# Regrouping the eight PSUM banks of the second half of an attention and mixture-of-experts kernel

## The chip, the cores and the metric

The kernel runs on one core of a Trainium2 chip. The metric is the device time of the program in microseconds, the median of several executions.

## The reference

The input is `x` of shape (2, 1024, 512) in float32: two sequences of 1024 tokens, 2048 tokens in all, each with 512 features. A vector per sequence, `c`, is multiplied with a matrix to give six modulation rows (shift, scale and gate for each of two halves).

The first half is a linear-attention layer: layer norm with modulation, a projection to queries, keys and values, a rotation of keys and values, a sum over all tokens of the products of normalized keys and values, and an output projection, added back through a gate.

The second half is a mixture of experts. With `h` the normalized and modulated tokens:

```
scores = softmax(h @ gate_w)                  # 8 experts, the best 2 of each token are used
g      = silu(h @ w_gate[e]) * (h @ w_up[e])  # hidden size 352, for each chosen expert e
routed = sum over the 2 experts of weight * (g @ w_down[e])
shared = (silu(h @ sw_gate) * (h @ sw_up)) @ sw_down      # hidden size 704, all tokens
out    = x + gate * (routed + shared)
```

## The kernel before, in words

Tokens are handled in 16 tiles of 128 (numbered `t`), and in four groups of four tiles (numbered `g`, 0 to 3). The first half of the program makes attention for all tokens, and, woven into it, the shared expert's hidden layer of group 0. What the change touches comes after that, in this order on TensorE:

1. **The rest of the shared expert for groups 0 and 1.** `shared_down(0, ...)` multiplies group 0's hidden layer with `sw_down`. Then `half_up(1, ...)` makes the last half chunk of group 1's hidden layer (tile `ph`, L1345), five calls of `seven(n, 1, ...)` make its five whole chunks, and `shared_down(1, ...)` makes its output (tiles `sd`, L928). `keep_shared` (L1044 on VectorE, L1045 on GpSimd) takes each output tile out of PSUM.
2. **The routed blocks.** Tokens sorted by expert are handled in blocks of 128 rows. Block `i` loads its rows (`hb`, L1417) and its expert's three weight matrices (`wg_r`, `wu_r`, `wd_r`), transposes the rows (`tr_b`, L337), makes two products (`bg` and `bu`, L1458), the gate on ScalarE and VectorE (L1336 to L1338), turns the result (`gtr`, L1470) and makes the output (`by`, L1486), which ScalarE copies out (L1490). How many blocks there are depends on the data: at least `NB0` = 32 and at most 39. The first 32 are plain code. Each later one stands in `tc.If(blocks > i)`, and the last block's output in `tc.If(blocks == i)` (L1578 and L1580), then `tc.If(blocks >= NB1)` (L1583) and one large conditional for the rest (L1586). In the profiled run 35 blocks are made, so blocks 32, 33 and 34 are in conditional code that runs, and the conditionals of L1583 and L1586 are passed by.
3. **The shared expert for groups 2 and 3.** Five pairs of `seven(n, 2, ...)` and `seven(n, 3, ...)`, two `half_up`, two `shared_down`. Between them VectorE adds the routed rows to the tokens (`next_sum`, L1377 to L1385).

`seven` makes a pair of 128x512 products with seven multiplications of 128x256 instead of eight (L1016). Each multiplication has two matmul instructions (one for each half of the inner dimension). They lie in four PSUM banks: `m1, m2` share one, `m6, m7` one, `m5, m3` one, and `m4` has one for itself. ScalarE copies `m1` (L1024), VectorE adds the others up (L1026 to L1034), ScalarE makes the sigmoid (L1036), VectorE multiplies (L1037, L1038).

From the second group of the shared expert on, the eight PSUM banks are two pools. A tile takes the next buffer of its pool in turn, and its first matmul waits until the earlier tile in that buffer has been read:

```python
    ps_mm = ctx.enter_context(tc.tile_pool(name="ps_mm2", bufs=5, space=PSUM))
    ps_tr = ctx.enter_context(tc.tile_pool(name="ps_tr2", bufs=3, space=PSUM))
```

`mm_ps` (five banks) holds `ph`, the three paired products of `seven`, and `bg`, `bu` and `by` of a block. `tr_ps` (three banks) holds `m4`, the outputs `sd` of `shared_down`, and the transposes `tr_b` and `gtr`.

The order of the instructions on each engine is not the order of the source. A scheduler lays them out when the program is built, by its own estimates of when operands and buffers are free. It can put an instruction ahead of others of its engine, also out of a later stage; it doesn't move one that touches a buffer which a conditional writes past that conditional. On the chip each engine then takes its instructions in the fixed order.

The weights of groups 2 and 3's shared expert are loaded a second time. Their first four chunks go into `s_again` (L1311), two transfers of 1 MB each, which SyncE issues among the first blocks' weights.

Of the kernel before, what the change touches and what calls it, by code (L numbers as in the profile page):

```python
# [8 lines left out]
FP = mybir.dt.float32  # L9
# [5 lines left out]
PSUM = bass.MemoryType.PSUM  # L15
# [3 lines left out]
P = 128  # L19
# [5 lines left out]
def kernel(  # L25
# [22 lines left out]
    E, _, H = w_gate.shape  # L48
# [4 lines left out]
    NS = NT // 4  # L53
# [32 lines left out]
    ps_mm = psums.enter_context(tc.tile_pool(name="ps_mm", bufs=3, space=PSUM))  # L86
    ps_tr = psums.enter_context(tc.tile_pool(name="ps_tr", bufs=2, space=PSUM))
# [9 lines left out]
    def mm_ps(name):  # L97
        return ps_mm.tile([P, 512], FP, tag="mm", name=name)

    def tr_ps(name):  # L100
        return ps_tr.tile([P, 512], FP, tag="tr", name=name)
# [5 lines left out]
    def act_tile(home, name):  # L107
# [11 lines left out]
        out=before_t,  # L119
# [687 lines left out]
    gTs = {}  # L807
# [92 lines left out]
    def shared_weights():  # L900

        tiles = [weight_tiles(f"s{i}a") for i in range(2)]
        wgu = []
        for i, (wg, wu, wd) in enumerate(tiles):
            views = []
            for w, src in ((wg, sw_gate), (wu, sw_up)):
                v = w.rearrange("p k h -> p (k h)").rearrange("p (k h) -> p k h", k=KH)
                nc.sync.dma_start(
                    v, src.rearrange("(k p) h -> p k h", p=P)[:, i * KH : (i + 1) * KH, :]
                )  # L910
                views.append(v)
            wgu.append(views)
        wds = load_down([wd for _, _, wd in tiles])

        def up_part(which, i, h0, m):
            return wgu[i][which][:, :, h0 : h0 + m]

        return up_part, wds

    def shared_down(g, gT, wds, use, ps_of, apart=False):  # L920


        for j0 in range(0, 4, 2):
            pss = [ps_of(f"sd_{g}_{j0 + i}") for i in range(2)]

            def chunk(i, c):
                rows = slice(i * HP, (i + 1) * HP) if c == NF else slice(0, P)
                nc.tensor.matmul(  # L928
                    pss[i],
                    gT[rows, c, (j0 + i) * P : (j0 + i + 1) * P],  # L930
                    wds[c][rows, :],
                    start=(c == 0),
                    stop=(c == NF),
                )

            if apart and j0 == 2:
                for i in range(2):
                    for c in range(NF + 1):
                        chunk(i, c)
            else:  # L940
                for i in range(2):
                    for c in range(NF):
                        chunk(i, c)
                    if i == 0:
                        yield
                for i in range(2):
                    chunk(i, NF)
            for i in range(2):
                use(g * 4 + j0 + i, pss[i])
            yield  # L950
# [37 lines left out]
    def mix_weights(n, up_part, store):  # L988

        a11, a12, a21, a22 = (  # L990
            up_part(w, i, n * P, P) for w in range(2) for i in range(2)
        )
        store = [v.rearrange("p (k h) -> p k h", k=KH) for v in store]
        s1, s2, s4 = store[0:3]
        s3 = store[3] if len(store) > 3 else a21
        nc.vector.tensor_add(s1, a21, a22)
        nc.vector.tensor_sub(s2, s1, a11)
        nc.vector.tensor_sub(s3, a11, a21)
        nc.vector.tensor_sub(s4, a12, s2)
        return a11, a12, a22, s1, s2, s3, s4  # L1000

    def seven(n, g, weights, b):

        a11, a12, a22, s1, s2, s3, s4 = weights
        c1, c2 = (
            gpool.tile([P, 2 * TH], FP, tag="sg", bufs=8, name=f"c{i}_{n}_{g}")
            for i in range(2)
        )
        (c11, c12), (c21, c22) = ((c[:, 0:TH], c[:, TH:]) for c in (c1, c2))

        def products(ps, *pairs):
            halves = []
            for i, (w, h) in enumerate(pairs):
                half = ps[:, i * TH : (i + 1) * TH]
                for k in range(KH):
                    nc.tensor.matmul(  # L1016
                        half, w[:, k, :], h[:, k, :], start=(k == 0), stop=(k == KH - 1)
                    )
                halves.append(half)
            return halves  # L1020

        add = nc.vector.tensor_add
        m1, m2 = products(mm_ps(f"m12_{n}_{g}"), (a11, b.b11), (a12, b.b21))
        nc.scalar.copy(c11, m1)  # L1024
        m6, m7 = products(mm_ps(f"m67_{n}_{g}"), (s2, b.t2), (s3, b.t3))
        add(c12, c11, m6)  # L1026
        add(c11, c11, m2)
        add(c22, c12, m7)
        m5, m3 = products(mm_ps(f"m53_{n}_{g}"), (s1, b.t1), (s4, b.b22))
        (m4,) = products(tr_ps(f"m4_{n}_{g}"), (a22, b.t4))  # L1030
        add(c12, c12, m5)
        add(c12, c12, m3)
        add(c21, c22, m4)
        add(c22, c22, m5)  # L1034
        dst = gTs[g][:, n, :]
        on_act = nc.scalar.activation(dst, c1, AF.Sigmoid)  # L1036
        nc.vector.tensor_mul(dst, dst, c1)  # L1037
        return on_act, nc.vector.tensor_mul(dst, dst, c2)  # L1038
# [227 lines left out]
    up_part, wds = shared_weights()  # L1266
# [26 lines left out]
    hroom.close()  # L1293
    attn.close()
    psums.close()
    ps_mm = ctx.enter_context(tc.tile_pool(name="ps_mm2", bufs=5, space=PSUM))
    ps_tr = ctx.enter_context(tc.tile_pool(name="ps_tr2", bufs=3, space=PSUM))


    gpool = ctx.enter_context(tc.tile_pool(name="gpool", bufs=1, side="right", reuse_waits="tile"))  # L1300
# [13 lines left out]
    def shared_again(firsts):  # L1314
        tiles = [weight_tiles(f"s{i}b") for i in range(2)]
        rests = []
        for w, src in zip(tiles[0], (sw_gate, sw_up)):
            v = w.rearrange("p k h -> p (k h)")[:, 0 : KC * (HS - HB)].rearrange(
                "p (k h) -> p k h", k=KC
            )  # L1320
            nc.sync.dma_start(v, src.rearrange("(k p) h -> p k h", p=P)[:, :, HB:HS])
            rests.append(v)
        wds = load_down([wd for _, _, wd in tiles])

        def up_part(which, i, h0, m):
            if h0 < HB:
                w = firsts[which]
            else:
                w, h0 = rests[which], h0 - HB
            return w[:, i * KH : (i + 1) * KH, h0 : h0 + m]  # L1330

        return up_part, wds
# [67 lines left out]
    for n in range(NF):  # L1400
        seven(n, 1, ready.pop(n), toks[1])
        if n + 2 < NF:
            ready[n + 2] = mix_weights(n + 2, up_part, s_stores[n % 2])
    for _ in shared_down(1, gTs[1], wds, keep_shared, tr_ps):
        pass


# [73 lines left out]
        return gtT  # L1481

    def block_out(i, gtT, w):
        ps = mm_ps(f"by_{i}")
        for c, (_, m) in enumerate(HCH):
            nc.tensor.matmul(  # L1486
                ps, gtT[:m, c, :], w[2][:m, c, :], start=(c == 0), stop=(c == NH - 1)
            )
        y = rpool.tile([P, D], FP, tag="y", name=f"y_{i}")
        nc.scalar.copy(y, ps)  # L1490

        queue = nc.sync if i + 1 < NB0 else nc.scalar
        queue.dma_start(ybuf[i * P : (i + 1) * P, :], y)
# [21 lines left out]
    def finish_block(i):  # L1515
        block_out(i, turned[i], weights[i])
# [83 lines left out]
    up_part, wds = shared_again(firsts)  # L1600
# [22 lines left out]
    for n in range(NF):  # L1623
        for g in last:
            after = seven(n, g, ready[n], toks[g])

            if n:
                next_sum(after)
        if n == 1:
            with tc.issue_after(after[1].ins):  # L1630
                ready[NF - 1] = mix_weights(NF - 1, up_part, quarters(s_last))
# [2 lines left out]
        next_sum()  # L1634
    spare = act_tile(4, "spare_again")
    for g in last:
        for _ in shared_down(g, gTs[g], wds, finish, tr_ps, apart=(g == NS - 1)):
            pass


# [67 lines left out]
```

## Time and profile before

| what | value |
|---|---|
| median of 3 runs | 771.56 us (768.81 to 772.03) |
| the profiled execution's own time | 772.12 us |
| its span, first to last instruction | 770.3 us |
| mean granted TensorE clock | 0.994 |
| TensorE busy | 751.9 us, 98% of the span |
| VectorE busy | 428.7 us, 56% |
| ScalarE busy | 232.5 us, 30% |
| GpSimd busy | 214.9 us, 28% |
| HBM traffic | 128.15 MB read, 30.16 MB written |

A timeline row gives the start, the length, the engine (PE is TensorE's matmul, PEld its weight load, DVE VectorE, ACT ScalarE, SPq the queue of SyncE), the source line, the operation, the tiles out and in, and how many executions the row merges. In brackets stands the idle time of the engine before it and what ended it. A float32 matmul instruction shows as two executions. Rows of matmuls overlap, since their ends are modelled: the distance between starts is the better measure. In a table of stretches each engine's busy time is followed by the number of instructions, then come the granted clock (PEclk; 1.00 is full), the share in which the DMA engines were busy, and GB/s.

### The profile page before, as it was taken

The page shows a single profiled execution, that of the slowest core. Times are in us where ns is not written, and L with a number is a line of the kernel's source. Part 1 is how long each engine was busy: PE and PEld are TensorE (multiplying, and loading weights), DVE is VectorE, ACT ScalarE, POOL GpSimd, SP SyncE. Part 2 cuts the span into 40 slices and gives each one's busy share as a digit, 9 for nine tenths or more (in the row PEclk, how much of TensorE's full clock was granted, in tenths as well). Part 3 has the DMA queues.
Part 4 walks back from the last instruction along what each step waited for, and adds up shares of the span by engine and source line. Part 5 has one row for each costly group of instructions (what it writes and reads, how often), then busy time and mean ns, then how long its engine had stood idle before and what let it go on. Part 6 is the DMA issues. An engine that isn't in the chain of part 4 may idle for free. (4 is left out here: it accounts for less than half of the span.)

```text
span 770.3 us, 8477 instructions
## 1 busy us (share of the span) xinstructions
PE 751.9 (98%) x2527; PEld 415.8 (54%) x2527; DVE 428.7 (56%) x979; ACT 232.5 (30%) x495; POOL 214.9 (28%) x241
## 2 busy tenths in 40 slices
PE   7999999999999999999999999999999998999997
PEld 2444444444444444684565656656566554888542
DVE  3888956898736888982222123222221121499964
ACT  4664523557643153110122122221221212122310
POOL 1234524863632687562100000000000000234530
PEclk9999999999999999999999999999999999999999
DMA  8950001212335711367999999999999884624551
GB/s 322 383 170 16 14 0 69 109 57 67 137 96 195 269 68 42 123 260 252 337 352 347 348 344 334 343 339 325 330 338 331 292 287 161 193 83 136 166 163 55
DMA packets 96369, 158.91 MB, mean 206 GB/s; under 512 B 8089, under 2 KB 51097, under 8 KB 96321
## 3 DMA queue, kind: packets, MB, share of 16 engines
q1 hardware_dynamic: 89984, 138.41, 53.6%
q0 software_dynamic: 5760, 18.88, 7.4%
q10 hardware_dynamic: 576, 1.05, 0.4%
q8 instruction: 22, 0.36, 0.2%
q14 instruction: 27, 0.21, 0.1%
HBM read 128.15 MB, written 30.16 MB: 206 GB/s over the span
## 5 line engine op out<-in xcount | busy, mean ns | idle before, releaser
L1360 POOL DMA_INDIRECT y<-ybuf,yrows x32 | 37.0, 1156 | 336.0 <-SPq L1586 288.4
L410 PE MATMUL kv<-w_kv,xnT 128*128 128x512 f32 x256 | 115.2, 596 | 0.5 <-ACT xnT L393 0.5
L1486 PE MATMUL by<-wd_r,gtT 128*128 128x512 f32 (+1 forms) x210 | 96.1, 593 | 0.8 <-DVEq L1578 0.8
L1458 PE MATMUL bg<-wg_r,hbT 128*128 128x352 f32 x280 | 88.9, 460 | 0.9 <-ACT y L1490 0.9
L1458 PE MATMUL bu<-wu_r,hbT 128*128 128x352 f32 x280 | 88.5, 459 | 0.0
L410 PEld LDWEIGHTS kv<-w_kv,xnT 128*128 128x128 f32 x256 | 46.9, 190 | 57.2 <-issue 48.1
L1458 PEld LDWEIGHTS bu<-wu_r,hbT 128*128 128x128 f32 x280 | 53.2, 190 | 29.6
L1473 DVE COPY gtT<-gtr 128x256 f32<-128x256 f32 x35 | 14.9, 425 | 97.0 <-PE gtr L1470 97.0
L1458 PEld LDWEIGHTS bg<-wg_r,hbT 128*128 128x128 f32 x280 | 50.4, 190 | 23.5 <-ACT y L1490 1.3
L571 PE MATMUL o<-wp,xnT 128*128 128x512 f32 x128 | 57.3, 593 | 0.0
L1337 DVE TENSOR_TENSOR sg_b<-sg_b,bg 128x352 f32<-128x352 f32 x35 | 18.3, 521 | 68.8 <-ACT sg_b L1336 68.8
L1486 PEld LDWEIGHTS by<-wd_r,gtT 128*128 128x128 f32 (+1 forms) x210 | 37.2, 191 | 34.5 <-issue 33.5
L1450 ACT COPY hbT<-tr_b 128x512 f32<-128x512 f32 x36 | 21.1, 586 | 101.1 <-PE tr_b L337 101.1
L1338 DVE TENSOR_TENSOR gt<-sg_b,bu 128x352 f32<-128x352 f32 x35 | 18.3, 521 | 47.2 <-PE bu L1458 47.2
L1490 ACT COPY y<-by 128x512 f32<-128x512 f32 x35 | 20.5, 586 | 70.7 <-PE by L1486 48.9
L571 PEld LDWEIGHTS o<-wp,xnT 128*128 128x128 f32 x128 | 23.8, 190 | 28.6 <-issue 27.0
L1336 ACT ACTIVATE sg_b<-bg 128x352 f32<-128x352 f32 x35 | 16.2, 464 | 76.1 <-PE bg L1458 76.1
L440 POOL TENSOR_TENSOR cross<-kv 128x128 f32<-128x128 f32 x16 | 12.6, 790 | 75.4 <-DVE kv L417 45.2
L530 PE MATMUL wp<-aw,wqT 128*128 128x512 f32 x64 | 30.0, 625 | 0.7 <-DVE aw L511 0.7
L433 ACT ACTIVATE sq<-kv 128x512 f32<-128x512 f32 x32 | 20.2, 630 | 27.2 <-DVE kv L417 25.6
L610 POOL TENSOR_TENSOR hr<-hr,cb 128x512 f32<-128x512 f32 x16 | 22.3, 1393 | 21.3 <-issue 7.2
L393 ACT ACTIVATE xnT<-tr_a,colsb 128x128 f32<-128x128 f32 x64 | 24.4, 455 | 11.0 <-PE tr_a L337 10.9
(319 smaller groups left out, 1264.7 us busy)
## 6 DMA issues: line engine op xcount, KB each, us to landing
wg_r<-in_w_gate_dram SPq DMA_DIRECT2D x35, 704.0 KB
wu_r<-in_w_up_dram SPq DMA_DIRECT2D x35, 704.0 KB
wd_r<-in_w_down_dram SPq DMA_DIRECT2D x35, 512.0 KB
hb<-hbuf SPq DMA_DIRECT2D x36, 256.0 KB
ybuf<-y SPq DMA_DIRECT2D x31, 256.0 KB
wd_r<-in_w_down_dram SPq DMA_DIRECT2D x35, 192.0 KB
wmod<-in_wmod_dram SPq DMA_DIRECT2D x6, 1024.0 KB
x<-in_x_dram SPq DMA_DIRECT2D x3, 1024.0 KB
```

Source lines behind the costliest of these rows:

```text
L393: turned1[t] = nc.scalar.activation(xnT[g][:, f, j * P : (j + 1) * P], ps[:, f * P : (f + 1) * P], AF.Identity, bias=colsb[:, 1, f : f + 1 ...
L410: nc.tensor.matmul(ps, xnT[g][:, k, j * P : (j + 1) * P], w_kv[:, i, k, :], start=(k == 0), stop=(k == KC - 1),)
L433: nc.scalar.activation(sq, kv[:, i, :], AF.Square, accum_out=ss[:, i : i + 1])
L530: nc.tensor.matmul(ps, wqT[:, k, f * P : (f + 1) * P], aw[:, k, :], start=(k == 0), stop=(k == KC - 1),)
L571: nc.tensor.matmul(ps, xnT[g][:, k, j * P : (j + 1) * P], wp[:, k, :], start=(k == 0), stop=(k == KC - 1),)
L610: nc.gpsimd.tensor_mul(h, h, cb1[b])
L1337: nc.vector.tensor_mul(sg[:m, :n], sg[:m, :n], pg[:m, :n])
L1360: nc.gpsimd.indirect_dma_start(out=y, out_offset=None, in_=ybuf, in_offset=bass.IndirectOffsetOnAxis(ap=yrows[:, t, s : s + 1], axis=0), b ...
L1450: nc.scalar.copy(hbT.rearrange("p k q -> p (k q)"), ps)
L1458: nc.tensor.matmul(ps[:, :H], hbT[:, k, :], wt[:, k, :], start=(k == 0), stop=(k == KC - 1))
L1486: nc.tensor.matmul(ps, gtT[:m, c, :], w[2][:m, c, :], start=(c == 0), stop=(c == NH - 1))
L1490: nc.scalar.copy(y, ps)
```

## The change

The eight banks become four pools of two: `mm_ps` keeps `ph`, `m5`/`m3`, `bg` and `bu`; `tr_ps` keeps `m4`, `tr_b` and `gtr`; `out_ps` takes `m6`/`m7` and the block outputs `by`; `start_ps` takes `m1`/`m2`. The output tiles `sd` of `shared_down` take two from `start_ps` and two from `tr_ps` in turn. No tile that is made inside a conditional comes from `start_ps`.

```diff
-        m1, m2 = products(mm_ps(f"m12_{n}_{g}"), (a11, b.b11), (a12, b.b21))
+        m1, m2 = products(start_ps(f"m12_{n}_{g}"), (a11, b.b11), (a12, b.b21))
         nc.scalar.copy(c11, m1)
-        m6, m7 = products(mm_ps(f"m67_{n}_{g}"), (s2, b.t2), (s3, b.t3))
+        m6, m7 = products(out_ps(f"m67_{n}_{g}"), (s2, b.t2), (s3, b.t3))
...
-    ps_mm = ctx.enter_context(tc.tile_pool(name="ps_mm2", bufs=5, space=PSUM))
-    ps_tr = ctx.enter_context(tc.tile_pool(name="ps_tr2", bufs=3, space=PSUM))
+    ps_mm = ctx.enter_context(tc.tile_pool(name="ps_mm2", bufs=2, space=PSUM))
+    ps_tr = ctx.enter_context(tc.tile_pool(name="ps_tr2", bufs=2, space=PSUM))
+    ps_out = ctx.enter_context(tc.tile_pool(name="ps_out", bufs=2, space=PSUM))
+
+    ps_start = ctx.enter_context(tc.tile_pool(name="ps_start", bufs=2, space=PSUM))
+
+    def out_ps(name):
+        return ps_out.tile([P, 512], FP, tag="out", name=name)
+
+    def start_ps(name):
+        return ps_start.tile([P, 512], FP, tag="start", name=name)
+
+    def down_ps():
+
+        turns = [start_ps, start_ps, tr_ps, tr_ps]
+
+        def ps_of(name):
+            turns.append(turns.pop(0))
+            return turns[-1](name)
+
+        return ps_of
...
-    for _ in shared_down(1, gTs[1], wds, keep_shared, tr_ps):
+    for _ in shared_down(1, gTs[1], wds, keep_shared, down_ps()):
...
-        ps = mm_ps(f"by_{i}")
+        ps = out_ps(f"by_{i}")
...
-        for _ in shared_down(g, gTs[g], wds, finish, tr_ps, apart=(g == NS - 1)):
+        for _ in shared_down(g, gTs[g], wds, finish, down_ps(), apart=(g == NS - 1)):
```

In the built program this moves instructions of TensorE, and little else. The first product pair `m1`/`m2` of groups 2 and 3 (eight matmul instructions, `m<-hT,s_again`) stood after all conditionals. Now one of them stands after the two first `tr_b` and ahead of block 0's `bg`, two stand behind block 31's `gtr` ahead of the load of the block count, and five between the conditional of L1583 and that of L1586. The one `m4` matmul of group 1 that stood ahead of `ph` goes back behind it. On SyncE some conditional weight loads of blocks past the 35th change places with row loads; on VectorE a few small operations of the block table change places with group 1's gate.

## The prediction

> **What bounds the kernel now.** I read the page first: TensorE is busy for 98% of the span, so only its gaps, its clock and waits newly put in its way can move the time. Less than 20 us are idle in all.
>
> ```profile
> span 770.3 us, 8477 instructions
> PE 751.9 (98%) x2527; PEld 415.8 (54%) x2527; DVE 428.7 (56%) x979; ACT 232.5 (30%) x495; POOL 214.9 (28%) x241
> ```
>
> Second, the timeline of TensorE around the places where the built order differs: the conditionals behind the blocks, the head of group 1's shared expert, and the passage from `sd` to block 0. First the conditionals:
>
> ```profile
> 649.64 0.49 PE L1470 MATMUL gtr<-ident,gt 128*128 128x128 f32 x3
> 650.98 2.81 PE L1486 MATMUL by<-wd_r,gtT 128*128 128x512 f32 x6 [0.84 <-DVEq L1578]
> 655.76 3.63 PE L1016 MATMUL m<-hT,s_again 128*128 128x256 f32 x8 [1.97 <-ACTq L1586]
> 659.19 2.84 PE L1016 MATMUL m<-t_store,s_room 128*128 128x256 f32 x12
> ...
> 663.59 1.89 PE L1016 MATMUL m<-hT,s_again 128*128 128x256 f32 x8
> ```
>
> The reader is to see two things. TensorE waits 0.84 and 1.97 us at conditionals. And the first `m1`/`m2` pair takes 659.19 - 655.76 = 3.43 us, where the same eight executions for group 3 take 1.73 (663.59 to 665.32). The table of stretches tells why. I cut it at the places where the granted clock changes; the clock has steps of 3.41 us:
>
> ```profile
> 96.16:99.57 3.41, 1.88 (x13) 1.61 (x14) 2.87 (x12) 2.24 (x6) 1.50 (x3) 1.00 0.00 0
> 99.57:102.98 3.41, 3.41 (x5) 1.21 (x4) 3.38 (x9) 2.73 (x8) 1.63 (x2) 0.50 0.00 0
> 649.11:652.52 3.41, 2.57 (x9) 1.23 (x8) 0.62 (x2) 0.59 (x1) 0.00 (x0) 1.00 0.21 79
> 652.52:655.94 3.42, 1.45 (x4) 0.39 (x4) 0.00 (x0) 0.59 (x1) 0.00 (x0) 1.00 0.20 72
> 655.94:659.36 3.42, 3.42 (x9) 2.67 (x10) 0.00 (x0) 0.00 (x0) 0.13 (x1) 0.50 0.05 14
> ```
>
> After a step in which TensorE was busy for 1.45 of 3.42 us (42%), or 1.88 of 3.41 (55%), the next step ran at half clock; after 2.57 (75%) it did not. A fully busy step at half clock costs 3.41/2 = 1.71 us.
>
> Third, the head of group 1:
>
> ```profile
> 312.64 0.37 PE L750 MATMUL count<-seen,ones_t 128*128 128x8 f32 x2
> 313.69 0.70 PE L1016 MATMUL m<-mixed,wu_s1a 128*128 128x256 f32 x2 [0.68 <-DVE spare L1044]
> 314.32 0.64 PE L1345 MATMUL ph<-hT,wg_s0a 128*64 128x512 f32 x1
> ```
>
> An `m4` matmul stands ahead of `ph` and waits for a bank that `keep_shared` is still reading. Fourth, the passage to block 0, on TensorE and on SyncE's queue:
>
> ```profile
> 367.37 0.66 PE L337 MATMUL tr_b<-ident,hb 128*128 128x128 f32 x4
> 368.29 0.66 PE L337 MATMUL tr_b<-ident,hb 128*128 128x128 f32 x4 [0.26 <-DVE spare L1044]
> 368.78 2.56 PE L1458 MATMUL bg<-wg_r,hbT 128*128 128x352 f32 x8
> ```
>
> ```profile
> 357.39 0.38 SPq L874 DMA_DIRECT2D wu_r<-in_w_up_dram  x1
> 357.89 1.92 SPq L1311 DMA_DIRECT2D s_again<-in_sw_gate_dram  x1
> ```
>
> `s_again` is issued behind the rows and weights of two blocks, and that decides my forecast.
>
> **The change part by part.** The work of TensorE stays the same, so the sum is of idle time and clock. One of the moved matmul instructions is 1.73/4 = 0.43 us.
>
> *Head of group 1.* `ph` now comes right behind `count` and has no wait on VectorE in the built order: about 312.95 instead of 314.32, 1.37 earlier. The `m4` matmul goes back, 0.43. Gain 0.94, so `sd` ends at 366.43 instead of 367.37. ScalarE and VectorE keep up: `m53` of the second `seven` now needs the bank of `ph`, read until 323.4, and comes at about 326.1.
>
> *From sd to block 0.* With two `tr` banks instead of three, both holding the last two `sd`, the first `tr_b` waits for the first L1044 and the second for the second. The two L1044 take 1.29 us and began 0.17 after the end of `sd` (367.54), so they run 366.60 to 367.89 and the `tr_b` start at about 367.33 and 367.96. TensorE would be free at 368.45.
>
> *The matmul ahead of block 0.* It reads `s_again` and takes its operands in its place in the queue; behind it stand `bg`, `bu` and all blocks. When does the transfer land? Issued from 352.33 on, ahead of it and with it: `hb` 2 x 256, weights 3 x 704 and 512 + 192, again 704, `s_again` 1024, together 5,056 KB or 5.18 MB. The stretches give 147, 329, 303 and 372 GB/s for the four steps of 4 us from 352, and 386 for 368 to 370: 5.0 MB by 369, 5.38 by 370. So on average it is through at 369.5, and the trace's landing stamps have the last of its sixteen parts at 370.86. Nothing in the change brings those transfers forward: they start behind the scattered rows of `hbuf`, and the DMA engines are busy without a break (share 0.98 to 1.06 from 356 on). So the matmul starts at about 370.95, and `bg` at 371.38 instead of 368.78: block 0 is **2.60 later**, the two gains and losses before it included. In the block stage TensorE has no wait from 368.8 to 632, so nothing of it is recovered.
>
> *The clock at block 0.* Between 366.43 and 370.95 TensorE is idle for 3.4 us, 2.5 of them in one piece. Here a rule of the Trainium skill speaks the other way: "TensorE: Matmul & The Clock Gate", section "Why this matters for your kernels", says that no idle gap over some 3 us is to be left, else the clock falls back to half. By that rule neither the 1.97 us gap of now nor the new one of 2.5 costs clock. The rows above differ: gaps of 0.84 and 1.97 were enough, and what counts is the busy share of a step. So I count it. I laid the steps over the new gaps at all phases, with a limit between 55% and 75%: a half-clock step follows in every one, the loss is 1.0 to 3.4 us, and I take the middle, **2.4**. By the skill's rule it would be 0.
>
> *Two matmuls ahead of the block count.* They cost 0.86 and fill the 0.43 us gap that block 32's `bg` shows (633.07, behind `gtr`): **+0.43**, between 0 and 0.86.
>
> *The conditionals.* From the end of `by` at 653.79 to the first `m6` (659.19) it was 5.40 us. Now: passing the first conditional, for which I take the 0.43 of the similar passage ahead of `bg` at 641.82; five matmuls, 2.16, with two plain jumps between them, some 0.1; and passing the big conditional, 0.43 again: 3.12. ScalarE doesn't hold it up: its `y` and its jumps took until 655.71, 1.92 behind `by`. So **-2.25**, if the clock stays up. The busiest gaps now leave about 70% of a step busy, in the unknown band between 55 and 75%; a half-clock step would give back 1.71. The 0.84 us before `by` stays.
>
> *The pair of group 3* is done earlier as well: **-1.73**.
>
> *The last stage.* Each bank is now used again after two `seven` instead of after five or three tiles. The tightest reuse is the second `ph`: it needs L1034 of the last `seven`, which ended at 720.47, and came at 721.56; margin 1.1 us. VectorE is 93% busy there (39.61 of 42.47 us from 678.00 to 720.47) with no wait on TensorE in that stretch, so it moves along with its own start. It costs 0; if VectorE lagged by 2 us more, 0.9. In `sd`, pairs are used again 10 us after they were read: 0. SyncE's and VectorE's swapped instructions lie in code that is passed by or ahead of slack: SyncE's next loads (658.49) are first read at 684.76, GpSimd's gathers (659.23) at 676.46.
>
> Sum: 2.60 + 2.40 + 0.43 - 2.25 - 1.73 = **+1.45 us**. The span goes from 770.3 to 771.75, the profiled execution's own 772.12 to 773.6. That execution is 0.56 above the median, so on the median's scale: 771.56 + 1.45 = **773.0**.
>
> **The rivals.**
>
> *Nothing holds up the early matmul* (the transfer lands in time, or what stands behind it goes on). Then block 0's `bg` comes at 368.88, +0.10, and no clock is lost there: 0.10 + 0.43 - 2.25 - 1.73 = -3.45, or 768.1. For it: that is what the order was laid out for. Against it: the landing stamp and the full DMA engines.
>
> *The wait is there but the clock holds*, as the skill's rule has it: 2.60 + 0.43 - 2.25 - 1.73 = -0.95, or 770.6. Against it stand the rows with 0.50.
>
> *The clock falls at both places*, slower by more than 0.5%. If a step boundary falls over 1.2 us ahead of 370.95, the step after it is under 64% busy itself, and the clock stays low for a second step: 3.41 instead of 2.4. If the step over the conditionals falls short too, 1.71 more: 1.45 + 1.0 + 1.71 = +4.2, or 775.7. Each us by which `s_again` lands later adds one. For it: the steps' phase is free, and a share of 55% was not enough once. Against it: five matmuls now lie in the gap.
>
> *The change doesn't do what it says*: the order of the built program shows the eight matmuls ahead of the conditionals, so I leave this at nothing.
>
> **How the numbers follow.** Wait and lost clock at block 0: 0.62, giving +0.5 to +3.3. Both places: 0.20. Wait without lost clock: 0.08. No wait: 0.10. About 0.5% (3.86 us) is what a measurement of this kernel can tell from no change; the three runs before lie within 3.2 us. Over it on the fast side lies only a better end of the no-wait case: 0.06. On the slow side the case of both places, not all of it, and a late landing: 0.19. Between: 0.75. The range reaches from the wait without lost clock, and some of the no-wait case, 769.0, to both places, 775.8. The likeliest case's own range is 772.0 to 774.9.
>
> **What would show it.** Right: in the profile after, the first `m<-hT,s_again` at 370 to 372 with an idle time of over 2 us in front, put down to a DMA; PEclk 0.50 for a step or two from about 370; `ph` at about 313; a gap under 1.2 us ahead of the first `m<-t_store,s_room`, at full clock. Wrong: `bg` of block 0 before 369.5, or `m53`, `ph` or `m` waiting for VectorE in the last stage.

## The result, and the profile after

The changed kernel takes 772.08 us in the median of 19 runs (768.98 to 775.11), the kernel before 769.74 in the median of 19 (768.81 to 772.19). The ratio is 1.0024 with a 95% interval of 1.0014 to 1.0035: 1.85 us more, between 1.1 and 2.7. The forecast was 773.0 and +1.45.

The profiled execution after took 772.29 us, with a span of 770.5 us. First the page: the span, and the busy time of each engine.

```profile
span 770.5 us, 8479 instructions
PE 751.3 (98%) x2527; PEld 415.8 (54%) x2527; DVE 426.3 (55%) x979; ACT 232.2 (30%) x495; POOL 215.4 (28%) x241
```

Little moved in these sums. So, as before, the timeline of TensorE at the places where the order differs. The head of group 1 and the passage to block 0:

```profile
311.97 0.37 PE L750 MATMUL count<-seen,ones_t 128*128 128x8 f32 x2
312.27 0.64 PE L1364 MATMUL ph<-hT,wg_s0a 128*64 128x512 f32 x1
...
366.67 1.25 PE L337 MATMUL tr_b<-ident,hb 128*128 128x128 f32 x8 [0.85 <-DVE spare L1044]
369.98 0.70 PE L1016 MATMUL m<-hT,s_again 128*128 128x256 f32 x2 [2.05 <-DMA s_again<-in_sw_gate_dram]
370.51 4.01 PE L1477 MATMUL bg<-wg_r,hbT 128*128 128x352 f32 x8
374.32 2.78 PE L1477 MATMUL bu<-wu_r,hbT 128*128 128x352 f32 x8
376.94 1.35 PE L1477 MATMUL bg<-wg_r,hbT 128*128 128x352 f32 x4
```

The reader is to see the order of the brackets: `ph` has no wait any more, `tr_b` waits 0.85 us for a bank, and the one matmul on `s_again` waits 2.05 us for a transfer, with all blocks behind it. Block 0's `bg` takes 4.01 us where it took 2.56. The table of stretches, cut at the clock's steps, says why:

```profile
367.99:371.40 3.41, 1.43 (x6) 1.06 (x6) 0.00 (x0) 0.55 (x1) 1.19 (x1) 1.00 1.05 387
371.40:374.82 3.42, 3.42 (x7) 2.01 (x6) 0.00 (x0) 0.20 (x1) 0.00 (x0) 0.50 1.07 307
```

TensorE was busy for 1.43 us of a step (42%), and the full step after it ran at half clock. The conditionals:

```profile
627.78 1.03 PE L1016 MATMUL m<-hT,s_again 128*128 128x256 f32 x4
...
655.56 2.85 PE L1505 MATMUL by<-wd_r,gtT 128*128 128x512 f32 x6 [1.10 <-ACTq L1599]
658.55 2.40 PE L1016 MATMUL m<-hT,s_again 128*128 128x256 f32 x10
661.10 2.83 PE L1016 MATMUL m<-t_store,s_room 128*128 128x256 f32 x12
```

The five matmuls follow the last `by` with almost nothing between, and the first `m6` stands 2.69 us behind the end of `by` (658.41), where it was 5.40.

The table below lays all profiled executions over one another. The beginning of the program differs by up to 2 us from one to the next, so times count from the start of `count` (L750), ahead of the changed code. "Block 1" is the start of block 1's `bg`; "last `by`" the start of block 34's `by`; the last column is the start of group 3's `m6`, by which every kernel has done the same eight matmuls on `s_again`. The ratios are those of the timed runs to the kernel before.

| kernel | ratio, 95% interval | `count` to block 1 | block 1 to last `by` | last `by` to first `m6` | `count` to group 3's `m6` |
|---|---|---|---|---|---|
| before | 1 | 60.90 | 277.44 | 8.21 | 352.68 |
| before, second profile | 1 | 60.90 | 277.43 | 6.62 | 350.99 |
| changed | 1.0024 (1.0014 to 1.0035) | 64.97 | 278.62 | 5.54 | 353.52 |
| e1_late | 0.9979 (0.9971 to 0.9987) | 60.87 | 278.56 | 5.11 | 349.79 |
| e2_early_load | 1.0015 (1.0003 to 1.0026) | 65.75 | 278.57 | 5.54 | 354.39 |
| e3_tr_first | 1.0031 (1.0020 to 1.0043) | 65.15 | 278.56 | 5.55 | 353.65 |
| e4_both | 0.9971 (0.9960 to 0.9983) | 59.95 | 278.62 | 5.11 | 348.94 |
| e5_no_room | 0.9991 (0.9983 to 0.9998) | 60.86 | 278.40 | 5.34 | 350.64 |
| e6_probe | 1.0027 (1.0014 to 1.0040) | 65.18 | 278.57 | 5.54 | 354.24 |
| e7_probe_fill | 1.0023 (1.0014 to 1.0033) | 64.39 | 278.57 | 5.54 | 353.32 |
| e8_probe_fill2 | 1.0012 (1.0004 to 1.0020) | 62.67 | 278.75 | 5.68 | 352.62 |
| e9_forced_load | 0.9980 (0.9970 to 0.9989) | 60.96 | 278.62 | 5.54 | 350.02 |
| e10_load_turns | 0.9966 (0.9957 to 0.9975) | 59.96 | 278.57 | 5.54 | 348.98 |

### The profile page after: what moved, and what is told of

Its sections match the earlier page's. It is cut to its first block, busy times and chain, and to the rows that moved or that the text cites. A ratio compares the mean times of both kernels' runs of the same rounds, so it can differ in the third digit from the quotient of the medians.

```text
span 770.5 us, 8479 instructions
## 1 busy us (share of the span) xinstructions
PE 751.3 (98%) x2527; PEld 415.8 (54%) x2527; DVE 426.3 (55%) x979; ACT 232.2 (30%) x495; POOL 215.4 (28%) x241
## 3 DMA queue, kind: packets, MB, share of 16 engines
q10 hardware_dynamic: 576, 1.05, 0.4%
```

## The experiments

A room is here a bank of one of the pools: the turning rooms are those of `tr_ps`, where block rows are turned (transposed), and the starting rooms those of `start_ps`. My theory was the forecast's main case: the matmul ahead of block 0 waits for `s_again`, and the gap then costs half the clock for a step. The rivals: the loss comes from having two turning rooms in place of three, or from the `sd` tiles in shared rooms; or the wait counts and the clock does not.

### The early matmuls held behind the blocks

e1_late keeps the rooms and changes only the order. Each m1/m2 matmul of the first pair of groups 2 and 3 gets an ordering dependence, without a semaphore, on block 31's last transpose:

```diff
+        if n == 0 and g > 1:
+            for ins in made:
+                tc.add_manual_dep(
+                    ins,
+                    last_turn[NB0 - 1].name,
+                    mybir.DependencyInfo(
+                        mybir.DependencyClass.NoSync, mybir.DependencyReason.DATA
+                    ),
+                    reason="behind the blocks",
+                )
```

> The rooms of the changed kernel stay; the m1/m2 matmuls of groups 2 and 3 of the first token part are held behind the blocks, so none stands ahead of block 0's bg. My theory (the matmul on s_again waits for its transfer, and the gap then halves the clock for one step): the wait of 2.05 us and its 0.35 us of work leave block 0, the half-clock step (1.7 us) with them, and 0.43 us comes back behind the conditionals: -3.7 us to the changed kernel, about 768.4 us, ratio to before 0.996 to 0.999; bg of block 0 starts near 368.5 (in the clock of the changed kernel's trace), no step at half clock near 371. Rival A (the loss comes from two turning rooms in place of three, or from the sd tiles): no gain, ratio 1.001 to 1.004. Rival B (the wait counts, the clock does not): -2.0 us, ratio near 1.000.

It took 768.18 us, ratio 0.9979. The passage to block 0 in its timeline:

```profile
365.04 1.25 PE L337 MATMUL tr_b<-ident,hb 128*128 128x128 f32 x8 [0.85 <-DVE spare L1060]
366.37 2.63 PE L1493 MATMUL bg<-wg_r,hbT 128*128 128x352 f32 x8
```

The 0.85 us ahead of `tr_b` is there as in the changed kernel, and `bg` follows at once and takes 2.63 us. From `count` to block 1 it is 60.87 us, as before the change (60.90). So the two turning rooms cost block 0 nothing beyond what the earlier `ph` gives, and its whole loss is bound to that one matmul. Without it the new rooms make the kernel 1.6 us faster than the one before (1.0 to 2.2 by the interval).

### One matmul put back, and its wait filled

e6_probe is e1_late with one matmul that reads `s_again` and writes a room nobody reads. (In the source it also turns block 1's rows ahead of that matmul; in the traces both turns stand there anyway. Elsewhere TensorE's order shifts only around the last blocks.) In e7_probe_fill four matmuls on the identity stand ahead of it, in e8_probe_fill2 two (`behind_of` is the ordering dependence of e1_late; the diff is that of e8_probe_fill2).

```diff
+    probe_ps = start_ps("probe")
+    after_ins = turned_in[-1]
+    for i in range(3):
+        probe = nc.tensor.matmul(
+            probe_ps[:, :256] if i == 2 else probe_ps,
+            firsts[0][:, 0, 0:P] if i == 2 else ident,
+            hT[2][:, 0, 0:256] if i == 2 else hT[2][:, 0, :],
+            start=True,
+            stop=True,
+        ).ins
+        behind_of(probe, after_ins)
+        after_ins = probe
...
+                if i == 0:
+                    behind_of(hidden, probe)
```

> The kernel with the held matmuls (e1_late) and one more matmul, on a quarter of s_again's gate part, into a room that nobody reads, placed between the two turns of block rows and block 0's bg. Theory: this one matmul alone brings the loss back: it waits about 2 us for s_again, bg of block 0 starts near 370.5, a half-clock step follows: +3.7 us to e1_late, about 772.1, ratio 1.001 to 1.004. Rival A: no more than its work, +0.35 us to e1_late. Rival B (wait, no clock loss): +2.4 us to e1_late.

> e6_probe with four 128x512 matmuls on the identity (1.76 us of work by the 0.44 of an sd matmul, result not read) ahead of the probe: they fill the wait, which still ends with s_again's landing. Theory (the clock falls because the step was too empty): bg of block 0 starts at the same time as in e6_probe, but at full clock: -1.7 us to e6_probe, about 770.4, ratio 0.999 to 1.002. Rival (the half step has another cause, or falls anyway): as e6_probe, 772.1.

> e7_probe_fill with two filling matmuls instead of four. A filling matmul of 128x512 took 0.86 us there (3.60 for four, since a product in this type is two instructions), so four outlasted the wait by 1.7 us and what the full clock brought went into that. Two take 1.72 of the 2.27 us that the probe waits. Theory: bg of block 0 starts with s_again's landing as in e6_probe and at full clock: 770.2 to 771.0, ratio 1.000 to 1.002, in mean -1.0 to -1.7 us to e6_probe. Rival (a lost step at half clock costs nothing that shows): 772.1, as e6_probe.

e6_probe: 772.08 us, ratio 1.0027; in the mean of its runs 772.06 against 768.24 for e1_late, so 3.8 us where 3.7 were expected. Its timeline and the stretches at the clock's steps:

```profile
369.86 0.70 PE L1569 MATMUL probe<-hT,s_again 128*128 128x256 f32 x2 [2.27 <-DMA s_again<-in_sw_gate_dram]
370.40 4.22 PE L1507 MATMUL bg<-wg_r,hbT 128*128 128x352 f32 x8
```

```profile
367.27:370.68 3.41, 1.14 (x6) 0.76 (x5) 0.00 (x0) 0.93 (x2) 1.58 (x2) 1.00 1.05 387
370.68:374.10 3.42, 3.42 (x7) 2.00 (x6) 0.00 (x0) 0.00 (x0) 0.00 (x0) 0.50 1.06 317
```

One matmul of 0.43 us brings back the whole loss, the half-clock step with it. With two filling matmuls (e8_probe_fill2):

```profile
367.83 1.88 PE L1569 MATMUL probe<-hT,ident 128*128 128x512 f32 x4
369.55 0.59 PE L1569 MATMUL probe<-hT,s_again 128*128 128x256 f32 x2
369.98 2.53 PE L1507 MATMUL bg<-wg_r,hbT 128*128 128x352 f32 x8
```

```profile
364.80:368.21 3.41, 2.56 (x14) 1.37 (x14) 1.29 (x2) 0.76 (x2) 1.44 (x2) 1.00 1.05 383
368.21:371.62 3.41, 3.41 (x12) 1.99 (x11) 0.00 (x0) 0.41 (x1) 1.05 (x1) 1.00 1.05 385
```

The work of nobody's use took the place of the idle time, the clock stayed at 1.00, and `bg` took 2.53 instead of 4.22 us. From `count` to block 1 that is 62.67 against 65.18: 2.51 us, 0.83 of it because `bg` also started earlier (57.93 behind `count`, against 58.76; the transfer had landed earlier in this execution). In e7_probe_fill the four took 3.60 us, so `bg` started 0.90 us later than in e6_probe (59.66 behind `count`) and block 1 came 0.79 us earlier (64.39): the full clock won back 1.69. In the timed runs I see less of it. e7_probe_fill took 771.89 us, ratio 1.0023: it is no faster than e6_probe, where its expectation had it faster by 1.7. One reason is my sizing, since I had taken a filling matmul for 0.44 us and it takes 0.86. e8_probe_fill2 took 771.52 us, ratio 1.0012, lower by 0.0015, about 1.2 us, and the intervals overlap; its profile also has waits of 0.38 and 0.54 us behind the conditionals, where e6_probe has one of 0.15.

The other reason lies in the mean clocks of the timed runs. A step at half clock takes 3.41/2 us out of 770, or 0.0022, off the mean clock. Of e6_probe's 18 runs, 7 have a mean clock of 0.995 or less, which is at least two such steps (9 of the 13 profiles have one near 99 us, in code that no edit touches), and 3 have 0.999, which leaves no room for any. Of the 17 runs of e7_probe_fill and the 22 of e8_probe_fill2 none is below 0.996. So filling the wait kept the clock in the timed runs too, and without it the step is lost in many executions and not in all. From the means (0.9961 in e6_probe, 0.9976 over the 55 runs of e1_late, e7_probe_fill and e8_probe_fill2) I estimate 0.7 lost steps per execution for the wait, taking the others to be lost as often.

### The transfer brought forward

e2_early_load exchanges two lines of source:

```diff
+    firsts = [shared_again_first(0)]
     weights = {0: block_weights(0)}
-    firsts = [shared_again_first(0), shared_again_first(1)]
+    firsts.append(shared_again_first(1))
```

> The changed kernel with the order of PE kept; only the transfer of s_again's gate part is issued ahead of block 0's weights instead of behind them. My theory: it lands near 364.5 instead of 369.9, the matmul ahead of block 0 runs without a wait, bg of block 0 starts near 368.9 instead of 370.5, the clock stays full: -1.7 and -1.7, about -3.4 us to the changed kernel, 768.7 us, ratio 0.997 to 0.999. The weights of block 0 land some 2.5 us later (wg_r near 366, wd_r near 369.7), still ahead of their use. Rival A (place in PE's order or rooms, not the transfer): no gain, ratio 1.001 to 1.004. Rival B (the later weights hold block 0 instead): wait on wg_r or wu_r, ratio 1.000 to 1.002.

It took 771.44 us, ratio 1.0015. On whether an earlier transfer helps it shows nothing, since the edit did not do what it should: the scheduler put the transfer where it was. SyncE's queue, and TensorE:

```profile
356.82 1.16 SPq L1330 DMA_DIRECT2D s_again<-in_sw_gate_dram  x1
```

```profile
368.76 1.22 PE L1016 MATMUL m<-hT,s_again 128*128 128x256 f32 x2 [1.47 <-DMA s_again<-in_sw_gate_dram]
369.77 4.90 PE L1477 MATMUL bg<-wg_r,hbT 128*128 128x352 f32 x8
```

The wait was shorter in this execution and the loss was larger, for the clock lay at half for two steps (368.15 to 374.98) instead of one. e9_forced_load ties block 0's `wg_r` to the transfer by an ordering dependence:

```diff
+        first = nc.sync.dma_start(wg, srcs[0].rearrange("(k p) h -> p k h", p=P))
+        if again and not again[1:]:
+            again.append(first)
+            tc.add_manual_dep(
+                first.ins,
+                again[0].ins.name,
+                mybir.DependencyInfo(
+                    mybir.DependencyClass.NoSync, mybir.DependencyReason.DATA
+                ),
+                reason="behind s_again",
+            )
```

> What e2_early_load was meant to do: there SyncE's queue kept its order, and s_again's gate part was issued at 356.8 as before. Now block 0's weights are held behind it, so it is the first after the two block rows; its up part follows block 0's weights. PE's order is that of the changed kernel. Theory: the gate part lands near 362, the matmul ahead of block 0 finds it there, bg of block 0 starts 2.0 us earlier, at full clock: -2.0 and up to -1.7, 768.4 to 769.5, ratio 0.998 to 1.000. Rival: block 0's weights, 1024 KB later, hold bg in its place (wait on wg_r or wu_r, 0.5 to 2.5 us): ratio 1.000 to 1.003.

```profile
352.58 0.40 SPq L1342 DMA_DIRECT2D s_again<-in_sw_gate_dram  x1
353.49 0.38 SPq L875 DMA_DIRECT2D wg_r<-in_w_gate_dram  x1
```

```profile
367.02 0.60 PE L1028 MATMUL m<-hT,s_again 128*128 128x256 f32 x2
367.45 2.53 PE L1498 MATMUL bg<-wg_r,hbT 128*128 128x352 f32 x8
```

768.57 us, ratio 0.9980. TensorE's order is that of the changed kernel, instruction for instruction; only the transfers change places, and this one is issued 3.8 us earlier (41.35 behind `count` instead of 45.13). The matmul finds its operand without a wait, block 0's later weights hold nothing up, and the clock stays full. So it is the landing, not the place in the order, that costs. One of its 14 timed executions took 2041.93 us; no profile was taken of it, and its cause is open.

### The wait ahead of the first turn

In group 1 the `sd` tiles take the turning rooms first and the starting rooms last (e3_tr_first: the changed kernel with this; e4_both: e1_late with it; e10_load_turns: e9_forced_load with it):

```diff
-    for _ in shared_down(1, gTs[1], wds, keep_shared, down_ps()):
+    for _ in shared_down(1, gTs[1], wds, keep_shared, down_ps(tr_ps, tr_ps, start_ps, start_ps)):
```

> The changed kernel with only the second edit of e4_both: in group 1 the sd tiles take the turning rooms first, so the first turn of block rows doesn't wait for VectorE. The matmul on s_again stays ahead of block 0. Theory: the 0.85 us wait ahead of tr_b goes, and the wait for s_again grows by as much, since the landing doesn't move: bg of block 0 starts when it did, and the step before it is as empty as before: 772.0, ratio 1.001 to 1.004. Rival (the turning rooms hold block 0): -0.8 us, ratio 1.000 to 1.002.

> e1_late, and in group 1 alone the sd tiles take the turning rooms first and the starting rooms last (in the changed kernel the other way round), so that the first turn of block rows finds a room that VectorE left 10 us ago. Theory: the 0.85 us that tr_b waits for VectorE (L1044) ahead of block 0 goes; bg of block 0 follows the last sd by 1.5 instead of 2.2 us: -0.7 us to e1_late, about 767.5, ratio to before 0.996 to 0.998. Rival (the copy of the turned rows, or the landing of the weights, is next to hold bg): no change against e1_late, 768.2.

> e9_forced_load with the same edit of the sd tiles as e4_both: no wait for s_again and none for VectorE ahead of tr_b, PE's order that of the changed kernel. Theory: with s_again there, the two waits no longer hide each other: bg of block 0 starts 0.6 to 0.85 us earlier than in e9_forced_load, 767.4 to 768.2, ratio 0.996 to 0.998. Rival (the weights of block 0, now later, or the copy of the turned rows hold bg): as e9_forced_load, ratio 0.998.

e3_tr_first: 772.46 us, ratio 1.0031, as slow as the changed kernel. Its row shows that the wait was passed on and not saved:

```profile
370.19 0.67 PE L1016 MATMUL m<-hT,s_again 128*128 128x256 f32 x2 [3.35 <-DMA s_again<-in_sw_gate_dram]
```

`tr_b` comes 0.92 us earlier (53.78 behind `count`, against 54.70), and the wait for `s_again` grows from 2.05 to 3.35. Where nothing waits for the transfer, the same edit shows: e4_both 767.97 us, ratio 0.9971 against 0.9979 for e1_late; e10_load_turns 767.57 us, 0.9966 against 0.9980 for e9_forced_load. In the traces block 1 comes 0.92 and 1.00 us earlier. In the timed runs that is 0.2 us for e4_both, where 0.7 were expected, and 1.0 for e10_load_turns, and in both pairs the intervals overlap: the gain is seen in the traces, and the times don't settle its size. e10_load_turns:

```profile
365.01 1.09 PE L337 MATMUL tr_b<-ident,hb 128*128 128x128 f32 x8
365.94 0.69 PE L1028 MATMUL m<-hT,s_again 128*128 128x256 f32 x2
366.46 2.53 PE L1498 MATMUL bg<-wg_r,hbT 128*128 128x352 f32 x8
```

Here the early matmul does what such a matmul can do: it fills the time between the turns and `bg`, which waits 0.24 us for ScalarE's copy of the turned rows in e4_both and not at all here. With 0.9957 to 0.9975 this version beats the kernel before and the changed kernel; e4_both, at 0.9960 to 0.9983, can't be told from it.

### The rooms without the early matmuls

In e5_no_room groups 2 and 3 take m1/m2 from the rooms of `bg` and `bu`, which conditionals write:

```diff
-        m1, m2 = products(start_ps(f"m12_{n}_{g}"), (a11, b.b11), (a12, b.b21))
+        m1, m2 = products((start_ps if g == 1 else mm_ps)(f"m12_{n}_{g}"), (a11, b.b11), (a12, b.b21))
```

> The changed kernel, but for groups 2 and 3 the products m1 and m2 are taken from the rooms that the conditional blocks write to, as before; group 1 keeps its new rooms. All eight early matmuls then stand behind the conditionals. Theory: no wait at block 0, as in e1_late, but the gap at the conditionals is empty again: in the traces so far, from the start of the last by to the first m6, less work and half clock, 0.8 us in the changed kernel and in e1_late, 2.2 in the kernel before, so +1.4 us to e1_late and in some executions 1.7 more for a half-clock step there: 769.6 to 770.5, ratio 0.999 to 1.001. Rival (the early matmuls at the conditionals bring nothing): as e1_late, 768.2, ratio 0.998.

769.55 us, ratio 0.9991: the ratio came as expected, but not by the step that I gave for it. The gap did not go back to what it was:

```profile
651.91 2.84 PE L1505 MATMUL by<-wd_r,gtT 128*128 128x512 f32 x6 [1.11 <-ACTq L1599]
655.45 1.97 PE L1016 MATMUL m<-hT,s_again 128*128 128x256 f32 x8 [0.69 <-PEq L1605]
657.25 2.75 PE L1016 MATMUL m<-t_store,s_room 128*128 128x256 f32 x12
```

TensorE waits 0.69 us for its own jumps, where the kernel before waits 1.97 us with ScalarE's jumps as releaser, though all eight matmuls stand behind the conditionals as they did there. What differs, among other rooms, is that `by` now has its own, so that the rooms of m1/m2 are no longer shared with the tile that ScalarE copies out last. From the last `by` to the first `m6` that is 5.34 us for four matmul instructions, against 6.62. The early matmuls bring e1_late only 0.23 more in this column (5.11). So most of what I had put down to them goes with the new rooms; that it is the room of `by` is my reading, as no run changes that room alone. The early matmuls pay in the block stage. e1_late, with two of them there (0.86 us of work), takes 278.56 from block 1 to the last `by`. e5_no_room takes 278.40 without them, so it spends 0.70 us more on the same work; 0.44 of that is a wait for `hbT` ahead of block 32's `bg`, which nothing fills there. By group 3's `m6` e5_no_room is 0.85 us behind e1_late, and by the first `sd` of the last stage 1.17; the timed runs say 1.37.

### The kernel before, profiled once more

> The kernel before once more, unchanged. The profiled execution so far lies above most of its timed ones (770.3 of span; the mean clock was 0.994 or 0.995 in about a third of 108 runs, 0.997 and above in the others). Theory: in most executions the step after the conditionals is at full clock, and the first m pair behind them takes 1.7 us instead of 3.43: from the end of the last by to the first m6 3.7 us instead of 5.40, span near 768. Rival (this step is always lost and the difference lies in the head of the kernel): 5.40 again.

This execution took 768.5 us, with a span of 766.6. Its timeline at the conditionals and the step there:

```profile
648.90 2.81 PE L1486 MATMUL by<-wd_r,gtT 128*128 128x512 f32 x6 [0.84 <-DVEq L1578]
653.68 1.99 PE L1016 MATMUL m<-hT,s_again 128*128 128x256 f32 x8 [1.97 <-ACTq L1586]
655.52 2.75 PE L1016 MATMUL m<-t_store,s_room 128*128 128x256 f32 x12
```

```profile
649.75:653.16 3.41, 1.97 (x5) 0.57 (x3) 0.00 (x0) 0.59 (x1) 0.00 (x0) 1.00 0.09 30
653.16:656.58 3.42, 2.90 (x13) 2.58 (x14) 0.00 (x0) 0.37 (x1) 0.18 (x1) 1.00 0.24 84
```

The waits of 0.84 and 1.97 us are the same to the hundredth, but the steps lie otherwise over them, the emptiest is 58% busy, and no half-clock step follows: 3.81 us from the end of `by` to `m6` instead of 5.40. Of the 158 runs of the kernel before that were timed beside the experiments, 46 had a mean clock of 0.994 or 0.995 and took 770.4 to 772.8 us; the others took 768.3 to 771.6. I read this as the step being lost in about three executions of ten; in the profiles it was seen in one of two. The mean clock doesn't say which step was lost, but its mean over the 158 runs (0.9970, against the 0.9976 above) gives the same estimate: some 0.3 lost steps per execution.

## Why the prediction was right, and where its terms were off

The mechanism was the one forecast, and e6_probe and e9_forced_load show it from both sides. By its steps, each from `count` and against the kernel before:

- *Head of group 1.* `ph` was to come 0.31 us behind `count`; it came at 0.30. Right.
- *From sd to block 0.* Block 0's `bg` was to be 2.60 us later; it is 2.40 (58.54 against 56.14 behind `count`). `tr_b` waits for the bank as said, the matmul for the transfer; that came about 0.2 us earlier than the stamp I used. e3_tr_first shows that the bank's wait is hidden in the transfer's.
- *The clock at block 0.* I set 2.4 us, between 1.0 and 3.4. In the profile block 1 is 4.07 us late, so the clock took 1.67: one step, not the mean over phases. In e2_early_load it was two steps. Over all its timed runs the changed kernel loses about 0.8 steps here, or 1.4 us, an estimate from its mean clock of 0.9958; and one run of the 19 has a mean clock of 0.999, so a step does not follow at every phase, as I had laid it out. The 55% in my limit was also a misreading: of the 1.88 us of the row for 96.16, 1.05 are products with a single column (last section). The rule of the Trainium skill ("TensorE: Matmul & The Clock Gate", "Why this matters for your kernels"), weighed in the prediction, would have set 0; a gap of 2.05 us was enough here, and filling it (e8_probe_fill2) kept the clock.
- *Two matmuls ahead of the block count.* I set +0.43, and it is +0.86. I had the gap of 633.07 ahead of the wrong block: there block 33's `bg` waits, and it still does (0.49 us, where it was 0.43). Ahead of block 32's `bg`, where the two stand, there was no gap to fill. The other 0.33 us of the 1.19 in the table are the wait ahead of the last `by`, 1.10 instead of 0.84, and the 0.06 that block 33's `bg` waits longer; I had both at nothing.
- *The conditionals.* I set -2.25 against the first profile, where -2.71 came (5.40 to 2.69): TensorE idles about 0.15 us at each of the two conditionals, ahead of 658.55 and of 661.10, where I had put 0.43. But 1.6 us of that is the half-clock step of the one profiled execution. Against the second profile it is -1.12 (3.81 to 2.69). This term was mis-sized for a typical execution: one profile showed a loss that seven in ten executions seem not to have, and I took it for the kernel's.
- *The pair of group 3.* Set at -1.73, found as -1.65 against the second profile (from the first `m6` to group 3's 6.04 us before and 4.39 after; it is the part of the table's last column that the three before it leave). Right.
- *The last stage.* Set at 0, and 0.8 us later by the trace: `sd` of it starts at 725.26 against 725.09 before, 0.84 later from `count`, as late as group 3's `m6` already was (353.52 against 352.68). So nothing is lost or won in between. Right.

The sum against the second profile is +4.07 + 1.19 - 1.08 - 1.65 = +2.53 us, and against the first +0.84. The runs say +1.85, between the two, as it should be if the kernel before loses its step in three executions of ten: 2.53 - 0.3 x 1.7 is 2.0, an estimate. With the changed kernel's step lost in only 0.8 of its executions it is 1.7. So the kernel before's first profile and the one after each show more lost clock than a typical execution has, and +1.45 came as close as it did partly by luck.

Against an execution of before without the lost step, the forecast's +1.45 is 1.1 short: the conditionals' gain was 1.2 too large and 0.8 was left out ahead of them, against which block 0 and its clock were 0.9 too dear. It came within 0.4 of the runs because the kernel before pays part of that step and the changed kernel doesn't always pay its own. The range of +0.5 to +3.3 for the likeliest case is not the sum of its terms either: with 1.0 to 3.4 for the clock they give +0.05 to +2.45. The level, 773.0 against 772.08, is too high although the rise was too small: it was laid on the median of three runs, 771.56, and that of all 19 is 769.74.

The gain that the rooms can bring was there, only hidden: the scheduler put a freed matmul into a hole ahead of block 0, and its operand landed 2 us too late for it. That the scheduler's estimates leave out how full the DMA engines are is my reading; no run shows it. With the hole left alone (e4_both) or the operand in time (e10_load_turns) the same rooms make the kernel 0.3% faster than before.

## What to carry to other kernels

Freeing a buffer lets the scheduler move work forward, so look at what each moved instruction reads and when that lands, before looking at the hole that it fills: an instruction that waits in an in-order queue holds up all that stands behind it. A gap on TensorE costs its own length and perhaps a step at half clock on top, which some matmuls of no use prevented here (e8_probe_fill2), at the price of the wait alone. Lay two profiles of the same kernel over each other before you take a loss in one of them for the kernel's own.

## What the runs showed of the hardware

The step's busy share, as the profile counts it, does not decide alone. Steps that were 34%, 42% and 50% busy ahead of block 0 were each followed by half clock, and one of 58% in the kernel before's second profile was not. But near 95 us, in code that no edit touches, a step of 2.12 of 3.41 us (62%) in e8_probe_fill2 was followed by half clock, and one of 2.11 in e1_late was not:

```profile
95.05:98.46 3.41, 2.12 (x14) 1.31 (x12) 2.87 (x11) 2.30 (x6) 0.90 (x2) 1.00 0.00 0
93.52:96.93 3.41, 2.11 (x6) 0.57 (x4) 3.38 (x11) 2.58 (x8) 0.73 (x1) 1.00 0.00 0
```

The two hold different work. The 2.11 us of e1_late are products of 128x512 (`kv`). Of the 2.12 us of e8_probe_fill2, 1.05 are `amix`, eight executions with a single column. The same `amix` lies in the step of the kernel before (96.16 to 99.57) from which the prediction took its 55%:

```profile
97.29 1.05 PE L474 MATMUL amix<-ones_t,acc 128*128 128x1 f32 x8 [1.30 <-DVE acc L471]
```

Leave the products of at most 32 columns out of the busy time, and the steps of all 13 traces, up to the program's last matmuls, fall into two groups. Of those at full clock, the 14 with TensorE busy for less than about half of the time (the highest is 1.70 of 3.41 us, at 364.74 in e2_early_load) were each followed by half clock, and none of the others was (the lowest is 1.72 us, at 96.79 in the kernel before's second profile). Counted with these products, a step of 74% was followed by half clock (96.40 in e7_probe_fill) and one of 53% was not (15.38 in e10_load_turns). This is found in the traces afterwards, and no run tests it. At the program's end it does not come out: of two steps of 59% one was followed by half clock (763.93 in the changed kernel) and one was not (762.02 in e5_no_room).

A half-clock step can also follow another: in e2_early_load the step after the empty one was itself only 2.80 us busy, at half clock, and the next one was at half clock too.
